# A four-layer attention and expert kernel: other steps for layer 0's exps and experts, more matmuls on ones, an int4 maximum by a transpose, other steps for layer 3's norm and last outputs

## The chip, the cores and the metric

The kernel runs on one core of a Trainium2 chip. The metric is the device time of one execution in microseconds. Three executions of the kernel before were timed, and one more was profiled. TensorE is called PE in the profile, VectorE DVE, ScalarE ACT, GpSimd POOL and SyncE SP; PEld is TensorE's weight load, which runs beside its matmuls.

## The reference

The input x has 16 sequences of 256 tokens of 128 numbers: 4096 tokens. There are four layers, each of the form `x = x + attention(xn) + ffn(xn)` with `xn` the layer norm of x.

```python
# layer 0: 16 heads of 8; each sequence keeps the 76 keys of largest importance
importance = relu(xn @ wi1.T + bi1) @ wi2.T + bi2
out = softmax(q k / sqrt(8), over the kept keys) @ v @ wo.T + bo
# its ffn: 8 experts, each takes the 512 tokens with its largest gate
top_scores, sel = top_k(softmax(xt @ wg).T, 512)
h = silu(routed @ w1) * (routed @ w3);  out[sel] += h @ w2
# layer 1: 16 heads of 64, causal mask of a window of 32 and 64 global tokens;
#   ffn: the two best of 8 experts for each token, relu squared
# layer 2: 4 heads of 32 with a distance mask that depends on the query; ffn of width 512, two gelus
# layer 3: 16 heads of 64, causal;  ffn: a matrix quantized to int4, plus a low-rank term
scale = max(|kernel|) / 7
w = clip(round(kernel / scale), -8, 7) * scale
y = xn @ w + bias + (xn @ a) @ b
```

## The kernel before, in words

All numbers are float32. The 4096 tokens are eight chunks of 512 (`NC = 8`), each of four tiles of 128 tokens. x stays on chip from layer to layer. The order of the work is written out by hand, in numbered steps, and each engine executes its instructions in the order in which the program issues them: an instruction that waits holds up everything behind it on its engine.

**PSUM** has eight banks: two tiles "sc" of two banks each, two "tp" of one, one "mm" and one "po". A tile is free again when its readers are done. `mm1()` gives the single "mm" bank, so every user of it waits for the one before; layer 0's `bank()` goes round "tp" and "mm".

**Layer 0** (`Layer0.run`) runs steps kk from -8 to 67, eight to a chunk (c = kk // 8, r = kk % 8). An even step issues `exps`: 16 matmuls of keys by queries (L817) into two "sc" tiles and two ACT exponentials (L823). An odd step issues `maxima` of the next chunk (16 matmuls L783 and four DVE reductions L789). Then come, as the step asks, `queries` (transposes of the maxima, L803, and a DVE addition L808), `outputs` of the exps one step earlier (L834, copied by ACT at L840), `divided` (transposes L849), `turned` (L864), `project` (L874, DVE addition L878) and `value` (L766). After these the step advances its lanes, which are generators: `prelude` (the choice of keys for a chunk two ahead, its ranking on DVE at L708 and L712), `choice` (15 rounds of a search for the experts' thresholds: a DVE comparison ge L485, matmuls L491 that count, DVE L496 to L502) and one `expert` for each e, which starts at step 19 + 3e. An expert builds one-hot tiles on DVE (L576, in two steps), multiplies them (L597) to get its token numbers (L605 to L610), gathers its rows with four indirect DMAs on POOL's queue (L613), scales them by their gates on DVE (L623), transposes them (L629), runs the two matrices (L638, silu L642, product L643), the third one (L648), copies the result y with ACT (L653; one buffer), and adds the rows to a tensor in HBM with four indirect DMAs on POOL's queue (L662). `fetch` reads that tensor back on SP's queue, `finish` (L998, POOL) adds it to the attention's result, and `Route.early` begins layer 1's norm (`stat`, `root`, `apply` L1292, `turn` L1298) while layer 0 ends. `warm(n)` issues n matmuls of a tile of ones by itself (L373), whose result nobody reads; they stand where TensorE would have little to do.

**Layers 1 and 3** share `Pipeline.slots`: NU = 128 slots u, each a pair of heads of one sequence. Two slots make one round: scores (L1110), DVE minima (L1125), ACT exps (L1136), POOL division (L1145), transposes (L1155) with DVE copies eT (L1156), values (L1169), projections of later heads (L1082, L1095). `out_half` multiplies eight tiles of heads by the output matrix into the "mm" bank (L1187; in layer 3 first L1185 with the int4 matrix) at slots with u % 8 equal to 1 and 5. `norm_steps` computes layer 3's norm of the next chunk from slot u % 16 == 3 on, one piece to a slot: statistics in two slots, root, POOL's `xn` (L1051) in two slots, and then transposes into the "mm" bank (L1059) and a copy by ACT (L1061). In layer 1, `Route` runs beside it: `places` works out where each token goes, `scatter` writes rows (64 indirect DMAs), `blocks` runs the experts on blocks of rows from slot 49 on, `gather` reads rows back from slot 93 on. From slot 56 on, `aside` advances small things for later layers by one step a slot, among them `quantized`: the int4 matrix. It takes the maximum of each row on DVE, and the maximum over the 128 partitions with `partition_all_reduce` on POOL (L1984).

**Layer 2** runs block by block; in its last one, layer 3's generator is advanced at hand-picked places (`beside`), so that layer 3's first norm is done there.

Of the kernel before, what the change touches and what calls it, by code (L numbers as in the profile page):

```python
# [19 lines left out]
P = 128  # L20
# [202 lines left out]
class Layer0:  # L223
# [245 lines left out]
    def choice(self):  # L469
# [9 lines left out]
        for i in range(15):  # L479
# [7 lines left out]

            self.warm(12 if i < 2 else 4)
            pc = self.bank()[:, : 3 * NE * 8]
# [80 lines left out]
    def expert(self, e):  # L570
# [31 lines left out]
        nc.scalar.activation(fourths, pix[:, :P], AF.Copy)  # L602
        yield

        nc.tensor.matmul(pix[:, P : P + 8], lhsT=fourths, rhs=self.eighths, start=True, stop=True)  # L605
# [12 lines left out]
        yield  # L618
        if e % 2 == 0:

            yield

# [257 lines left out]
    def begin(self):  # L880
# [36 lines left out]
        for _ in lane:  # L917
# [5 lines left out]
        return {  # L923
            -8: [(self.stats, 6, 2, 6), (self.stats, 7, 2, 6), (self.root, 2, 6), (self.apply, 2), (self.apply, 3), warm],
            -7: [
# [7 lines left out]
    def run(self, tail):  # L933
# [7 lines left out]

        warm = {kk: 5 for kk in range(-8, 4)} | {kk: 2 for kk in range(12, 22)} | {kk: 3 for kk in range(53, 64)}
        loads = 19 + 3 * NE + 8
        for kk in range(-8, 8 * NC + 4):
            c, r = kk // 8, kk % 8
            if r == 0 and 0 <= c + 2 < NC:
                lanes.insert(0, self.prelude(c + 2))
                next(lanes[0])
            if 0 <= c < NC and r % 2 == 0:
                self.exps(c, r // 4, r // 2 % 2)  # L950
            if 0 <= c + 1 < NC and r % 2:
# [15 lines left out]
            if r >= 6 and 0 <= c + 1 < NC:  # L967
                self.value(c + 1, r - 6)
            if kk == 45:

                self.pg = self.k.po()
# [39 lines left out]
class Pipeline:  # L1011
# [25 lines left out]
    def norm_steps(self, c):  # L1037
# [12 lines left out]
        for t in range(TT):  # L1050
            nc.gpsimd.tensor_scalar(  # L1051
                xn[:, t, :], x[:, t, :], mv[:, t, 0:1], y[:, t : t + 1], ALU.subtract, ALU.mult
            )
            if t == 1:
                yield
        yield
        pt = k.mm1()
# [120 lines left out]

    def out_half(self, s, t, wo, first=None):

        k, nc = self.k, self.k.nc
        p = k.mm1()
        if first is not None:
            t0 = s % 2 * S + t * P
            nc.tensor.matmul(p[:, :D], lhsT=self.xnT[s // 2][:, t0 : t0 + P], rhs=first, start=True, stop=False)  # L1185
        for n in range(8):
            nc.tensor.matmul(  # L1187
                p[:, :D], lhsT=self.oT[s][:, n, t * P : (t + 1) * P], rhs=wo[:, n, :],
                start=(first is None and n == 0), stop=(n == 7),
            )  # L1190
        return p[:, :D]

    def slots(self, extra, mid=None):

        if self.own:
            yield
            yield from self.norm_steps(0)
            yield
# [55 lines left out]
class Route:  # L1254
# [71 lines left out]
    def early(self):  # L1326

        at = {}
        for first, n in ((0, 2), (2, 2), (4, 2), (6, 1)):
            for c in range(first, first + n):  # L1330
                u = 57 + c + c // 6
                at.setdefault(u, []).append((self.stat, c, first, n))
                for late, step in ((0, self.apply), (1, self.turn)):
                    at.setdefault(59 + c + late, []).append((step, c))
        at[64].append((self.gates, 0))
# [5 lines left out]
    def last(self):  # L1341
        c = NC - 1
        yield
        self.stat(c, c, 1)
        yield
        self.root(c, 1)
        self.apply(c)
        yield
        self.turn(c)
        yield  # L1350
        self.gates(c - 3)
        yield
        self.others(c - 3)
# [198 lines left out]
def layer1(k, wk_, w, route, l2, aside, warm):  # L1552
# [15 lines left out]
    def extra(u):  # L1568
# [9 lines left out]
        next(first, None)  # L1578
        for g, at, n in ((0, 15, 2), (1, 93, 2)):
            if u == at:  # L1580
                rows[g] = route.gather(range(EARLY)) if g else route.scatter()
            if g in rows:
                for _ in range(n):
                    next(rows[g], None)
        if 0 <= u - 49 < NB // 2:
            lanes.append(route.blocks(2 * (u - 49)))
        mid(u)
# [25 lines left out]
class Layer2:  # L1613
# [266 lines left out]
    def run(self, wk_, att, begin, l3, route):  # L1880
# [20 lines left out]
        for n in range(NC + 1):  # L1901
# [38 lines left out]
            beside(1)  # L1940
            do(self.turn, q)
            do(self.first, f, 3)
            beside(1)
            do(self.third, f - 1, 0)
# [26 lines left out]
def quantized(k, pool, a):  # L1971
# [9 lines left out]
    nc.vector.tensor_reduce(m, kw, AX.X, ALU.max, apply_absolute_value=True)  # L1981
    yield
    mx = pool.tile([P, 1], F32, name="q_mx")
    nc.gpsimd.partition_all_reduce(mx, m, P, bass_isa.ReduceOp.max)  # L1984
    yield
    yield
# [4 lines left out]
    yield  # L1991
    q = pool.tile([P, D], F32, name="q_q")
    nc.vector.tensor_scalar(q, kw, inv[:, 0:1], None, ALU.mult)
# [15 lines left out]
def layer3(k, wk_, sh, room, w, xs, out):  # L2009
# [9 lines left out]
    pipe = Pipeline(k, wk_, xs, (w["Wq"], w["Wk"]), w["Wv"], k.causal, home=home)  # L2019
    res = {}  # L2020

    def extra(u):
        for late, t in ((9, 0), (13, 1)):
            s, at = (u - late) // 8, (u - late) % 8
            if at or not 0 <= s < 2 * NC:
                continue
            c, n = s // 2, s % 2 * 2 + t
            if n == 0:
                res[c] = k.xp.tile([P, TT, D], F32, tag="x", name="res")
            p = pipe.out_half(s, t, w["o"], first=w["eff"])  # L2030
            nc.vector.tensor_tensor(res[c][:, n, :], p, w["bias"], ALU.add)
            nc.gpsimd.tensor_tensor(res[c][:, n, :], res[c][:, n, :], xs[c][:, n, :], ALU.add)
            if n == 3:
                nc.sync.dma_start(out[c * CT : (c + 1) * CT, :].rearrange("(t p) d -> p t d", p=P), res[c])

    yield from pipe.slots(extra)
# [154 lines left out]
```

## Time and profile before

| what | value |
|---|---|
| three timed executions | 1952.15, 1945.82, 1943.68 us (median 1945.82) |
| the profiled execution, its time and its span | 1939.03 us, 1937.3 us |
| mean granted TensorE clock in it | 0.985 |
| layer 0's exps, L823 | x64, 61.4 to 355.4 us |
| layer 1's values, L1169 on p_v | x1024, 388.2 to 981.3 us |
| layer 2's blocks, L1811 | x512, 1007.2 to 1389.4 us |
| layer 3's values, L1169 on m | x1024, 1405.8 to 1924.9 us |
| POOL's maximum for the int4 matrix, L1984 | x1, 377 ns, at 657.9 us |
| matmuls on ones, L373 | x346, 1.0 to 374.5 us |
| POOL's gathers of layer 0, L613 | x32, median 956 ns, landing 2.6 us after the issue |
| POOL's scatters of layer 0, L662 | x32, median 1574 ns, landing 3.4 us after the issue |

In the profile, a line such as "x<-a,b" names the tile that is written and those that are read. "idle before" is the time in which an engine did nothing before an instruction, with what ended it. Matmuls overlap: one of 0.27 us can follow its forerunner after 0.11 us, so their pitch is read from start to start. The share of the clock that is granted to TensorE stands in windows as a number from 0 to 1.

### The profile page before, as it was taken

How to read it: one execution, taken by the hardware profiler on the slowest of the kernel's cores; microseconds unless marked ns; L12 is line 12 of the kernel's file. 1: busy time of each engine (PE TensorE's matmuls, PEld its weight loads, DVE VectorE, ACT ScalarE, POOL GpSimd, SP SyncE). 2: the span in 40 equal slices, each digit the busy share in tenths (PEclk: the TensorE clock that was granted, in tenths of full speed). 3: DMA queues.
4: the chain of work that ended last, by engine and by line, in shares of the span. 5: the costliest groups of instructions: out<-in, count | busy, mean ns of one | idle time of the engine just before them, and what ended most of it. 6: DMA issues, size and time to landing. Idle time of an engine off the chain costs nothing.

```text
span 1937.3 us, 39257 instructions
## 1 busy us (share of the span) xinstructions
PE 1850.1 (95%) x13823; PEld 1335.7 (69%) x13823; DVE 1226.1 (63%) x4819; ACT 1052.8 (54%) x3162; POOL 960.8 (50%) x1388
## 2 busy tenths in 40 slices
PE   9998889889999899999999999999999999999998
PEld 5555455568878788887754555555577877877786
DVE  6888664697665555568765555443277667766765
ACT  4334545656666566666644444444466666666664
POOL 4015776337997466565664444421144444444442
PEclk9989999899999999999999999999999999999999
DMA  8500223200014354300010000000000000000000
GB/s 248 145 1 13 30 30 66 74 1 23 33 34 129 101 140 136 88 20 15 16 41 5 9 10 12 12 1 1 1 1 8 1 7 7 7 1 7 7 1 12
DMA packets 83208, 72.28 MB, mean 37 GB/s; under 512 B 14466, under 2 KB 74020, under 8 KB 82852
## 3 DMA queue, kind: packets, MB, share of 16 engines
q1 hardware_dynamic: 66784, 38.01, 6.9%
q0 software_dynamic: 15488, 31.61, 6.7%
q8 instruction: 109, 1.79, 0.4%
q14 instruction: 87, 0.71, 0.1%
q10 hardware_dynamic: 740, 0.17, 0.0%
HBM read 49.70 MB, written 24.25 MB: 38 GB/s over the span
## 4 chain that ended last, share of the span: by engine, by line
PE 64%; DVE 7%; POOL 7%; issue 2%; ACT 1%; POOLq 0%; ACTq 0%; DVEq 0%
PE sc L1811 11%; PE sc L1082 9%; PE po L1169 7%; PE tp L1155 7%; PE sc L1110 7%; PE mm L1187 5%; PE sc L1095 4%; POOL e L1145 3%; POOL xb L1452 2%; DVE e L1125 2%; PE po L1511 2%; PE mm L1498 2%; PE mm L1851 2%; DVE eT L1156 1%; PE sc L1803 1%
## 5 line engine op out<-in xcount | busy, mean ns | idle before, releaser
L1145 POOL TENSOR_TENSOR e<-e,rs 128x256 f32<-128x256 f32 (+2 forms) x512 | 400.0, 807 | 483.1 <-DVE rs L1143 448.3
L1136 ACT ACTIVATE e<-e,mn 128x128 f32<-128x128 f32 (+2 forms) x1024 | 442.4, 434 | 285.8 <-DVE mn L1125 281.8
L1156 DVE COPY eT<-tp 128x384 f32<-128x384 f32 x512 | 261.3, 552 | 59.8 <-PE tp L1155 59.6
L1811 PE MATMUL sc<-ff,h 128*128 128x512 f32 x512 | 227.2, 593 | 1.6 <-DVE l_mn L1738 1.6
L1155 PE MATMUL tp<-ident,e 128*128 128x128 f32 x1536 | 219.0, 278 | 8.6 <-POOL e L1145 5.6
L1175 DVE COPY oT<-po 128x512 f32<-128x512 f32 x128 | 88.3, 690 | 215.8 <-PE po L1169 215.8
L1155 PEld LDWEIGHTS tp<-ident,e 128*128 128x128 f32 x1536 | 173.3, 141 | 61.6 <-issue 37.3
L1136 ACT ACTIVATION_READ_ACCUMULATOR e<-e,mn 128x1 f32 x1024 | 191.9, 187 | 0.0
L1811 PEld LDWEIGHTS sc<-ff,h 128*128 128x128 f32 x512 | 94.4, 190 | 106.4 <-issue 101.2
L1125 DVE CUSTOM_DVE_ANT_0 e<-sc,causal 128x128 f32<-128x128 f32 (+1 forms) x512 | 151.8, 353 | 11.2 <-PE sc L1110 10.8
L1125 DVE CUSTOM_DVE_ANT_0 e<-sc,sparse 128x128 f32<-128x128 f32 (+1 forms) x512 | 138.8, 328 | 7.2 <-POOL dist L183 2.2
L1082 PE MATMUL sc<-m,qkv 128*128 128x256 f32 x512 | 126.8, 390 | 1.7 <-DVE mn L1125 1.7
L1691 POOL TENSOR_SCALAR n<-dist,reach 128x128 f32<-128x128 f32 (+1 forms) x128 | 119.2, 931 | 16.4 <-DVE l_mn L1738 5.0
L1187 PE MATMUL mm<-out,oT 128*128 128x128 f32 x1024 | 124.9, 275 | 0.0
L1187 PEld LDWEIGHTS mm<-out,oT 128*128 128x128 f32 x1024 | 119.4, 192 | 0.1
L1790 POOL TENSOR_TENSOR x<-l_o,x 128x256 f32<-128x256 f32 x16 | 11.6, 727 | 199.7 <-DVE l_o L1784 199.3
L1082 PEld LDWEIGHTS sc<-m,qkv 128*128 128x128 f32 x512 | 92.5, 190 | 17.0 <-DVE mn L1125 2.3
L1110 PE MATMUL sc<-n 64*128 64x128 f32 (+1 forms) x1024 | 101.5, 337 | 1.3 <-ACT n L1087 0.8
L1169 PE MATMUL po<-eT,p_v 128*64 128x256 f32 (+1 forms) x1024 | 99.4, 333 | 2.0 <-DVE eT L1156 1.9
L1169 PE MATMUL po<-eT,m 128*64 128x256 f32 (+1 forms) x1024 | 98.1, 332 | 0.4 <-DVE eT L1156 0.4
L1169 PEld LDWEIGHTS po<-eT,p_v 128*64 128x64 f32 x1024 | 63.9, 136 | 43.7 <-issue 16.3
L1742 ACT ACTIVATE p_e<-p_e,l_mn 128x128 f32<-128x128 f32 (+1 forms) x128 | 56.3, 441 | 68.3 <-DVE l_mn L1738 68.1
(433 smaller groups left out, 3686.6 us busy)
## 6 DMA issues: line engine op xcount, KB each, us to landing
xb<-zero SPq DMA_DIRECT2D x1, 4608.0 KB, 20.4
xb<-xb SPq DMA_DIRECT2D x36, 128.0 KB, 2.8
yb<-yb SPq DMA_DIRECT2D x36, 128.0 KB, 2.3
x<-in_L_attn_x SPq DMA_DIRECT2D x8, 256.0 KB, 3.8
m<-in_L_ffn_w SPq DMA_DIRECT2D x8, 256.0 KB, 11.3
xn_d<-x SPq DMA_DIRECT2D x8, 256.0 KB, 8.0
m<-acc_d SPq DMA_DIRECT2D x8, 256.0 KB, 5.4
h<-in_L_ffn_h_wT SPq DMA_DIRECT2D x2, 1024.0 KB, 7.5
```

The lines of the kernel that those rows point to most:

```text
L1082: nc.tensor.matmul(p[:, n, i * S : (i + 1) * S], lhsT=self.wqk[n][:, (2 * gg + i) * P : (2 * gg + i + 1) * P], rhs=(self.xk if n else self ...
L1110: nc.tensor.matmul(ps[:, j, c0:c1], lhsT=qk[r, 0, i, qt * P : (qt + 1) * P], rhs=qk[r, 1, i, k0 : k0 + c1 - c0], start=True, stop=True,)
L1125: nc.vector.tensor_tensor_reduce(out=e[:, j, c0:c1], in0=ps[:, j, c0:c1], in1=self.mask[:, c0:c1], scale=1.0, scalar=3e38, op0=ALU.add, op ...
L1136: nc.scalar.activation(e[:, j, c0:c1], e[:, j, c0:c1], AF.Exp, bias=mn[:, n], scale=-1.0, accum_out=sums[:, n])
L1145: nc.gpsimd.tensor_tensor(e[:, :, c0:c1], e[:, :, c0:c1], bcast(rs[:, 2 * qt : 2 * qt + 2], 2, c1 - c0), ALU.mult)
L1155: nc.tensor.transpose(pt[:, n * P : (n + 1) * P], e[:, j, c0 : c0 + P], k.ident)
L1156: nc.vector.tensor_copy(eT[:, j, :], pt[:, :384])
L1169: nc.tensor.matmul(o[64 * j : 64 * j + 64, t * P :], lhsT=v[:, t ^ self.swap, h : h + 64], rhs=eT[:, j, t * S : t * P + S], start=(t == 0) ...
L1175: nc.vector.tensor_copy(self.oT[s][:, 2 * gg : 2 * gg + 2, :].rearrange("p i s -> p (i s)"), self.po.pop(g))
L1187: nc.tensor.matmul(p[:, :D], lhsT=self.oT[s][:, n, t * P : (t + 1) * P], rhs=wo[:, n, :], start=(first is None and n == 0), stop=(n == 7),)
L1691: self.nc.gpsimd.tensor_scalar(mk[:, j, c0:c1], self.k.dist[:, c0:c1], reach[:, g, t : t + 1], 1e18, ALU.is_gt, ALU.mult)
L1811: self.nc.tensor.matmul(ph, lhsT=self.w[wh][:, c, m * P : (m + 1) * P], rhs=src[c], start=(c == 0), stop=(c == NF - 1))
```

## The change

1. Layer 0: `exps` is issued behind the transposes and matmuls of an even step instead of ahead of them. An odd expert waits one step before it works out its numbers and gathers, and then has two free steps instead of one before it scales; an even expert keeps its steps. The fetches begin two steps later, as does the use of "po" for the ones of the end.
2. More ones: 28, 12 and then 7 in the rounds of `choice` instead of 12, 12 and then 4; 25 instead of 3 in step -8; 5 instead of 2 in steps 12 to 16.
3. `turn` of layer 1's early norm comes two steps after `apply` instead of one (also in `Route.last`), and scatter, blocks and gather begin one slot later.
4. `quantized` takes the maximum over the partitions by a DVE copy of the column to 128 columns, one PE transpose and a DVE maximum.
5. Layer 3's `norm_steps` has an empty slot between POOL's last piece and the transposes; its first norm starts one `beside` earlier, and one `beside` of layer 2 comes one block earlier.
6. Layer 3's result tile is begun by POOL with x plus the bias (one instruction of 128x512 for a chunk instead of four of 128x128 behind the DVE addition). The outputs of the last sequence are begun in slots 126 and 127 with six of eight tiles of heads, in the "mm" and a "tp" bank, and finished in slot 128.

```diff
@@ choice
-            self.warm(12 if i < 2 else 4)
+            self.warm((28, 12, 7)[min(i, 2)])
@@ expert
         nc.scalar.activation(fourths, pix[:, :P], AF.Copy)
         yield
+        if e % 2:
+            yield
...
         yield
         yield
-        if e % 2 == 0:
-
-            yield
+
+        yield
@@ Layer0.begin, run
-            -8: [..., (self.apply, 3), warm],
+            -8: [..., (self.apply, 3), (self.warm, 25)],
...
-        warm = {kk: 5 for kk in range(-8, 4)} | {kk: 2 for kk in range(12, 22)} | {kk: 3 for kk in range(53, 64)}
-        loads = 19 + 3 * NE + 8
+        warm = {kk: 5 for kk in range(-8, 4)} | {kk: 5 for kk in range(12, 17)} | {kk: 2 for kk in range(17, 22)} | {kk: 3 for kk in range(53, 64)}
+        loads = 19 + 3 * NE + 10
...
-            if 0 <= c < NC and r % 2 == 0:
-                self.exps(c, r // 4, r // 2 % 2)
...
             if r >= 6 and 0 <= c + 1 < NC:
                 self.value(c + 1, r - 6)
-            if kk == 45:
+            if 0 <= c < NC and r % 2 == 0:
+
+                self.exps(c, r // 4, r // 2 % 2)
+            if kk == 47:
@@ norm_steps, before its transposes
+        yield
         yield
         pt = k.mm1()
@@ slots
         if self.own:
-            yield
             yield from self.norm_steps(0)
@@ Route.early
-                    at.setdefault(59 + c + late, []).append((step, c))
+                    at.setdefault(59 + c + 2 * late, []).append((step, c))
@@ Route.last
         self.apply(c)
+        yield
         yield
         self.turn(c)
@@ layer1
-        for g, at, n in ((0, 15, 2), (1, 93, 2)):
+        for g, at, n in ((0, 16, 2), (1, 94, 2)):
...
-        if 0 <= u - 49 < NB // 2:
-            lanes.append(route.blocks(2 * (u - 49)))
+        if 0 <= u - 50 < NB // 2:
+            lanes.append(route.blocks(2 * (u - 50)))
@@ Layer2.run
             do(self.turn, q)
+            beside(1)
             do(self.first, f, 3)
-            beside(1)
@@ quantized
+    q = pool.tile([P, D], F32, name="q_q")
+    nc.vector.tensor_copy(q, m.to_broadcast([P, D]))
+    yield
+    pm = k.mm1()
+    nc.tensor.transpose(pm[:, :P], q, k.ident)
     mx = pool.tile([P, 1], F32, name="q_mx")
-    nc.gpsimd.partition_all_reduce(mx, m, P, bass_isa.ReduceOp.max)
-    yield
+    nc.vector.tensor_reduce(mx, pm[:, :P], AX.X, ALU.max)
     yield
@@ out_half
-    def out_half(self, s, t, wo, first=None):
+    def out_half(self, s, t, wo, first=None, p=None, upto=8):
-        p = k.mm1()
-        if first is not None:
+        begun = p is not None and upto == 8
+        if p is None:
+            p = k.mm1()
+        if first is not None and not begun:
...
-        for n in range(8):
+        for n in range(6, 8) if begun else range(upto):
@@ layer3, extra
+        if u == NU - 2:
+            last.append(k.mm1())
+        if u == NU - 1:
+            last.append(k.tp())
+        if u in (NU - 2, NU - 1):
+            pipe.out_half(2 * NC - 1, u - NU + 2, w["o"], first=w["eff"], p=last[-1], upto=6)
...
             if n == 0:
+
                 res[c] = k.xp.tile([P, TT, D], F32, tag="x", name="res")
+                nc.gpsimd.tensor_tensor(res[c], xs[c], bcast(w["bias"], 1, TT), ALU.add)
             p = pipe.out_half(s, t, w["o"], first=w["eff"])
-            nc.vector.tensor_tensor(res[c][:, n, :], p, w["bias"], ALU.add)
-            nc.gpsimd.tensor_tensor(res[c][:, n, :], res[c][:, n, :], xs[c][:, n, :], ALU.add)
+            nc.vector.tensor_tensor(res[c][:, n, :], p, res[c][:, n, :], ALU.add)
...
+        if u == NU:
+            c = NC - 1
+            for t in range(2):
+                p = pipe.out_half(2 * NC - 1, t, w["o"], p=last[t])
+                nc.vector.tensor_tensor(res[c][:, 2 + t, :], p, res[c][:, 2 + t, :], ALU.add)
+            nc.sync.dma_start(out[c * CT : (c + 1) * CT, :].rearrange("(t p) d -> p t d", p=P), res[c])
```

## The prediction

> **What bounds the kernel now.** I read the page first, then the chain of waits, then windows and timelines around each place that the change touches.
>
> ```profile
> span 1937.3 us, 39257 instructions
> PE 1850.1 (95%) x13823; PEld 1335.7 (69%) x13823; DVE 1226.1 (63%) x4819; ACT 1052.8 (54%) x3162; POOL 960.8 (50%) x1388
> PEclk9989999899999999999999999999999999999999
> PE 64%; DVE 7%; POOL 7%; issue 2%; ACT 1%; POOLq 0%; ACTq 0%; DVEq 0%
> ```
>
> TensorE is 95% busy and 64% of the chain, so a microsecond in which it stands still is mostly a microsecond of the total. The clock row dips only in its first fifth. Windows of one microsecond show it at 0.50 from 30.0 to 36.9, 112.0 to 118.8, 135.9 to 142.7, 176.8 to 183.7 and 347.5 to 354.3 (6.8 us each), at 211, 252, 272 and 378 (3.4 us each), and from 664.9 to 671.8. All but the last lie in layer 0 or at its end. So the change is a sum over TensorE's gaps and its half-clock stretches.
>
> **Part 1, the int4 maximum (layer 1's slot 60).** The timeline of that place:
>
> ```profile
> 657.87 0.38 POOL L1984 PARTITION_ALL_REDUCE q_mx<-q_m  x1 [5.76 <-issue]
> 666.01 1.44 POOL L1145 TENSOR_TENSOR e<-e,rs 128x256 f32<-128x256 f32 x2 [7.77 <-issue]
> 666.67 0.47 PE L1155 MATMUL tp<-ident,e 128*128 128x128 f32 x1 [4.78 <-POOL e L1145]
> ```
>
> The reduction takes 0.38 us, but POOL stands idle 5.76 us before it and 7.77 us after it, with nothing to wait for; TensorE then waits 4.78 us for POOL's division L1145 and falls to half clock. Windows from one pair of slots to the next (cut where the first L1169 of a pair starts) give the price:
>
> ```profile
> core 0: us, PE busy (x) PEld busy (x) DVE busy (x) ACT busy (x) POOL busy (x), PEclk, DMA share, GB/s
> 654.48:673.09 18.61, 13.46 (x94) 11.52 (x93) 9.00 (x31) 7.34 (x24) 6.65 (x10) 0.82 0.24 66
> 686.89:697.75 10.86, 10.86 (x93) 9.51 (x92) 6.44 (x25) 7.34 (x24) 5.47 (x9) 1.00 0.35 102
> ```
>
> The same work takes 18.61 instead of 10.86: 7.75 us. The next pair takes 13.80 where its like take 12.65; I count half of that 1.15, since the int4 steps stay in it: 8.3. What comes instead: a DVE copy of 128x128 (about 0.3, as L1577), one transpose (0.11 from start to start) and a DVE maximum. The transpose needs the single "mm" bank just after ACT's L1504; the like case is L2003, which waited 0.5 us for it. The maximum's own wait holds up DVE's next oT copy, which comes later than that anyway. Net **-7.7**, between -9 and -6.
>
> [...]
>
> **Part 2, layer 3's norm one step later.** Slots of the first chunk with this step, TensorE, then ACT:
>
> ```profile
> 1500.09 0.38 PE L1059 MATMUL mm<-ident,m 128*128 128x128 f32 x2
> 1500.77 0.33 PE L1059 MATMUL mm<-ident,m 128*128 128x128 f32 x1 [0.30 <-POOL m L1051]
> 1501.55 0.33 PE L1059 MATMUL mm<-ident,m 128*128 128x128 f32 x1 [0.44 <-POOL m L1051]
> 1501.71 1.89 PE L1082 MATMUL sc<-m,qkv 128*128 128x256 f32 x8
> 1504.10 0.39 PE L1185 MATMUL mm<-weff,m 128*128 128x128 f32 x2
> ...
> 1501.91 0.60 ACT L1061 ACTIVATE m<-mm 128x512 f32<-128x512 f32 x1 [0.82 <-PE mm L1059]
> 1504.16 1.00 ACT L1087 ACTIVATE n<-sc 128x1024 f32<-128x1024 f32 x1
> ```
>
> The last two transposes wait for POOL: starts 0.56 and 0.78 apart instead of 0.11, so 1.1 us. In all, seven chunks have a pair of 10.65 us against 9.13. One step later POOL is done. But step 9 also starts an output half (L1185), which uses the same single bank: its first matmul now waits for ACT's copy of the transposes, and that copy now stands behind step 8's exps and L1087. Worked out: without the step, L1082 starts at 1500.1; in a pair without a norm, L1087 ends 3.95 us after L1082 starts (1483.84 to 1487.79), so at 1504.05; plus 0.60 for the copy, 1504.65. Without a wait, transposes and outputs would stand at 1503.05. The new stall is about 1.6 against 1.1 now: +0.5 a chunk, seven times **+4**. Behind it in TensorE's queue stand L1095 and L1169, so nothing fills it. If ACT comes 0.5 sooner it is 0; 1 us later, +8.
>
> Before layer 3 proper, the same copy (1370.43) held TensorE's L1851 by 1.4 us; now block 3 of "first" (3.44 us) lies between: **-1.4**.
>
> **Part 3, the last outputs.** The end:
>
> ```profile
> 1930.21 0.29 DVE L2031 TENSOR_TENSOR res<-mm,bias 128x128 f32<-128x128 f32 x1 [2.37 <-PE mm L1187]
> 1930.58 0.45 POOL L2032 TENSOR_TENSOR res<-res,x 128x128 f32<-128x128 f32 x1 [2.21 <-DVE res L2031]
> 1931.06 0.37 SPq L2034 DMA_DIRECT2D out_dram<-res  x1
> ```
>
> Fourteen of the eighteen last matmuls go ahead of the last values, into idle time: from 1921.39 to 1930.17 TensorE idles about 1.9, of which I let 0.8 stay (the copy L1175 of 0.69 and its wait). POOL's 0.48 leaves the end. **-1.5**, between 0 and -3. POOL's four additions of 0.45 become one of 128x512 (1.26, as L998) ahead of the DVE addition, in POOL's queue behind a division; in step 9 that ends near when TensorE's half does, and DVE has slack: 0.
>
> **Part 4, layer 0.** Its TensorE gaps sum to 39.9 us, not all curable. Four rows:
>
> ```profile
> 32.03 1.46 PE L425 MATMUL tp<-ident,x 128*128 128x128 f32 x4 [3.39 <-ACT x L411]
> 176.83 1.12 PE L629 MATMUL mm<-ident,xr 128*128 128x128 f32 x4 [2.80 <-DVE qa L808]
> 228.07 0.69 DVE L623 TENSOR_TENSOR xr<-xr 128x512 f32<-128x512 f32 x1 [4.21 <-DMA xr<-xn_d,ids]
> 250.30 0.60 ACT L653 ACTIVATE y<-tp 128x512 f32<-128x512 f32 x1 [6.65 <-DMA acc_d<-y,ids]
> ```
>
> *Ones.* 92 more (22 at step -8, 16+39 in the choice, 15 in steps 12 to 16) at 0.11 from start to start are 10 us. The 22 (2.4 us) sit before the 3.39 us gap; the 16 before a wait of 2.34 for DVE's ge; the others beside a VectorE that is 85% busy. What stays on the path, I put at 1 to 2. They can save the stretches at 30, 112 and 136. [...] A stretch of 6.8 us costs at most 3.4, as half the matmuls go through. I take -1 for the first and -1.5 net for each of the others: **-4**, between -8 and +2.
>
> *Experts.* An odd expert's gather is issued one step later, its scaling (L623) two. Now the scaling of experts 3, 5 and 7 waits 4.2, 3.0 and 3.0 for the gather, because POOL has an expert's four scatters (about 7.7 us) ahead of it in the same slot; after, the gather goes first. TensorE lost 2.1 by the first, under 1 by the others: -3. The wait of ACT's copy y for the previous scatters (4.76 and 6.65; TensorE's part 1.8 and 2.7) moves from four pairs of experts to three: -1. The 2.80 before 176.83 hangs on VectorE's order, which stays. The last scatters end two slots later; SP's fetch (324.1, POOL adding from 327.0 to 334.8) moves with its users, two slots of 2.5. **-4**, -10 to +6.
>
> *Exps behind the transposes.* Work of 0.4 to 1.7 us goes ahead of exps that wait 7.6 us in all for banks; behind, the outputs have 1.2 to 6 us of slack after ACT's exps until slot 54, but only 0.05 to 0.6 later. Saved perhaps 2, lost perhaps 2: **0**, -3 to +4. Turns one slot later cure waits of 1.3 and 2.5 on ACT, but ACT itself waits there for VectorE's root: 0. The shifts by one slot in layer 1 (64 row scatters on POOL, the blocks' fetches on SP and weight gathers on POOL, 24 gathers) move together, each behind the same neighbours: 0, ±2.
>
> **Sum.** -7.7 +4 -1.4 -1.5 -4 -4 = -14.6. From the profiled execution's 1939.0 (span 1937.3 and 1.7 around it) 1924.4; the median shown is 1945.8, 6.8 higher, and I predict there: **1931**.
>
> **Rivals.** (a) *POOL takes over in layer 0, slower.* Slots 32 to 35 now hold a gather, scatters, a gather, scatters: 25 us of POOL (a gather about 5) in 23 (slots of 5.8). If ACT's y in slots 34, 40 and 46 waits a full 7.7 plus 3.4 to land, TensorE stops 4 to 5 us and then runs a 6.8 us stretch at half (3.4 lost): 7 to 8 for each pair, +23 for three and the -4 gone: 1958. From 5 us a pair on, it cancels all the rest. For it: ACT waited 6.65 so already. Against: two of four pairs had no such wait. (b) *Only the reduction's gain remains.* The ones save no stretch (+4), experts nothing (+4), the norm costs +8 (+4): 1943. For it: the single bank. (c) *Layer 0 gains more*: all its stretches at half clock after 112 go (another 10): 1921. Against: those at 176 and 347 begin with waits that stay.
>
> **Chances and range.** Forecast 0.58, (a) 0.12, (b) 0.17, (c) 0.13. The part bounds give 1916 to 1946 around the forecast; reaching into (a) and (c), 1913 to 1952. A change under 0.5% (9.7 us) can't be told from none: faster by more than that 0.69, within 0.18, slower 0.13.
>
> **What would show it.** No PARTITION_ALL_REDUCE and no second stop; the pair near 655 at about 11.5. L1185's first matmul with a wait for ACT in seven chunks, those pairs at 11 or more: if they are 10 or less, Part 2 is wrong. L623 without waits for DMA; 438 ones instead of 346, no half clock at 112 and 136. ACT's y waiting over 7 us three times would mean (a).

## The result and the profile after

| kernel | median (lowest to highest) | ratio to before, 95% interval | profiled span |
|---|---|---|---|
| before | 1945.77 us (1943.68 to 1952.15) | | 1937.3 us |
| changed | 1954.7 us (1951.35 to 1961.9) | 1.0046 [1.003, 1.0062] | 1952.0 us |

The changed kernel is 0.46% slower, 9 us, and the interval leaves out 1. The forecast was 1931 us. The first lines of its page:

```profile
span 1952.0 us, 39365 instructions
PE 1864.2 (96%) x13916; PEld 1346.7 (69%) x13916; DVE 1227.6 (63%) x4821; ACT 1052.2 (54%) x3162; POOL 959.2 (49%) x1363
PEclk9999897999999999999999999999999999999999
```

TensorE is busy for 14.1 us more, about the whole difference of the spans. The 92 more ones take some 8 of them. Busy time also holds what matmuls lose at half clock (the 16 of L818 take 1.10 us at full clock, at 59.69, and 2.00 at 0.50, at 309.80), but that explains little here: before the last issue the changed kernel spends 58.0 us at 0.50, the kernel before 54.6. I did not trace the rest. The clock row has its dip of 7 in the seventh slice, from 293 to 342 us, where the kernel before shows a 9.

Where the time goes is seen by taking the same matmul in both traces and subtracting its starts. Positive means that the changed kernel is late. I call this number the lag.

| same work | before, us | changed minus before, us |
|---|---|---|
| layer 0, exps of step 20 | 148.0 | -2.9 |
| step 42 | 277.8 | -6.9 |
| step 48 | 309.1 | +0.7 |
| step 52 | 321.0 | +10.9 |
| step 60 | 342.5 | +19.2 |
| layer 1, first values | 388.2 | +16.9 |
| the pair before the int4 pair | 641.8 | +17.2 |
| behind the int4 pair | 673.1 | +10.2 |
| layer 1, last pair | 980.1 | +13.5 |
| layer 3, first values | 1405.8 | +13.5 |
| layer 3, pair 62 | 1919.9 | +17.9 |
| end | 1937.3 | +14.7 |

Everything behind layer 0 sums to 14.7 - 16.9 = -2.2 us. All of the loss, and more, is in layer 0, and there between steps 42 and 60.

The int4 maximum did what was forecast. Windows of the changed kernel over the pair ahead of it and the pair that had taken 18.61 us:

```profile
core 0: us, PE busy (x) PEld busy (x) DVE busy (x) ACT busy (x) POOL busy (x), PEclk, DMA share, GB/s
659.01:672.46 13.45, 12.98 (x111) 11.39 (x110) 6.72 (x28) 7.29 (x24) 8.37 (x11) 1.00 0.47 135
672.46:683.32 10.86, 10.86 (x93) 9.51 (x92) 7.58 (x31) 7.34 (x24) 5.59 (x8) 1.00 0.40 106
```

The second pair is at its usual 10.86, without half clock. The first takes 13.45 against 12.65; this 0.80 is the price of the copy, the transpose and the maximum, and it is the same 13.45 in e4, which makes this change alone.

Layer 3's norm gives the stall that the prediction named. The timeline of the changed kernel in the first such chunk:

```profile
1516.90 0.60 PE L1062 MATMUL mm<-ident,m 128*128 128x128 f32 x4
1517.38 1.00 ACT L1090 ACTIVATE n<-sc 128x1024 f32<-128x1024 f32 x1
1518.28 0.58 ACT L1064 ACTIVATE m<-mm 128x512 f32<-128x512 f32 x1
1518.91 0.49 PE L1190 MATMUL mm<-weff,m 128*128 128x128 f32 x2 [1.41 <-ACT m L1064]
```

The four transposes follow each other without a wait, ACT copies their bank only behind its copy L1090, and the first output matmul waits 1.41 us for the bank. The same wait of 1.40 to 1.41 stands in all seven chunks.

In layer 0, ACT's copy y of expert 6 waits in step 46, and TensorE waits behind it. Timeline of the changed kernel:

```profile
308.11 0.60 ACT L654 ACTIVATE y<-tp 128x512 f32<-128x512 f32 x1 [4.98 <-DMA acc_d<-y,ids]
308.60 0.38 ACT L841 ACTIVATE ov<-mm 128x256 f32<-128x256 f32 x1
308.76 1.11 PE L850 MATMUL tp<-ident,ov 128*128 128x128 f32 x4 [2.79 <-ACT y L654]
```

ACT waits for the scatters of expert 5, which is now only two steps ahead of expert 6. TensorE's transposes of ov wait behind it, and from 308.17 to 321.8 the granted clock is 0.50. That looked like the answer; the experiments say that it is at most a part of it.

### The profile page after: what moved, and what is told of

It reads as the page before. It is cut to its first block, busy times and chain, and to the rows that moved or that the text cites. A ratio compares the mean times of both kernels' runs of the same rounds, so it can differ in the third digit from the quotient of the medians.

```text
span 1952.0 us, 39365 instructions
## 1 busy us (share of the span) xinstructions
PE 1864.2 (96%) x13916; PEld 1346.7 (69%) x13916; DVE 1227.6 (63%) x4821; ACT 1052.2 (54%) x3162; POOL 959.2 (49%) x1363
## 4 chain that ended last, share of the span: by engine, by line
PE 65%; DVE 6%; POOL 6%; ACT 2%; issue 1%; ACTq 0%; DVEq 0%
PE sc L1816 11%; PE sc L1085 9%; PE po L1172 8%; PE sc L1113 7%; PE tp L1158 7%; PE mm L1192 5%; PE sc L1098 4%; POOL xb L1457 3%; POOL e L1148 2%; PE mm L1503 2%; PE po L1516 2%; PE mm L1856 2%; PE sc L1808 1%; PE sc L1809 1%; DVE e L1128 1%
## 5 line engine op out<-in xcount | busy, mean ns | idle before, releaser
L1113 PE MATMUL sc<-qk 64*128 64x128 f32 (+1 forms) x1024 | 92.1, 320 | 5.9 <-ACT qk L1090 5.9
```

The costliest lines, as they stand in the source:

```text
L1113: nc.tensor.matmul(ps[:, j, c0:c1], lhsT=qk[r, 0, i, qt * P : (qt + 1) * P], rhs=qk[r, 1, i, k0 : k0 + c1 - c0], start=True, stop=True,)
```

## The experiments

Each ratio is to the kernel before, timed beside the run. One thousandth of a ratio is 1.95 us. The medians of e8, e11, e16 and e18 rest on 6 or 7 executions, the others on 11 to 22. "Layer 0" is my estimate of layer 0's part of the difference: ratio minus 1, times 1946, less what the later layers differ in the two profiles; the sign ± gives half the width of the ratio's interval. e4 and e8, whose layer 0 is the kernel before's, stand at 0 and -2 in it, which is how well the estimate does.

| run | edit | median, us | ratio [95%] | layer 0, us |
|---|---|---|---|---|
| e1 | changed, exps ahead | 1948.67 | 1.0010 [1.0001, 1.0019] | +4 ±2 |
| e2 | changed, old experts | 1949.15 | 1.0014 [0.9993, 1.0035] | +5 ±4 |
| e3 | changed, old norm step | 1953.86 | 1.0029 [1.0019, 1.0039] | +12 ±2 |
| e4 | before + int4 | 1939.62 | 0.9966 [0.9957, 0.9976] | 0 ±2 |
| e5 | changed, exps ahead, old experts | 1944.98 | 0.9992 [0.9978, 1.0005] | 0 ±3 |
| e6 | before + exps | 1945.57 | 1.0001 [0.9988, 1.0015] | -2 ±3 |
| e7 | before + experts | 1951.67 | 1.0023 [1.0011, 1.0035] | +3 ±2 |
| e8 | before + int4 + end | 1938.30 | 0.9949 [0.9931, 0.9968] | -2 ±4 |
| e9 | changed + second y | 1951.15 | 1.0037 [1.0019, 1.0055] | +9 ±4 |
| e10 | before + exps + experts | 1954.53 | 1.0051 [1.003, 1.0073] | +11 ±4 |
| e11 | e8 + exps before step 44 | 1927.86 | 0.9916 [0.9884, 0.9947] | -8 ±6 |
| e12 | e8 + second y | 1933.95 | 0.9944 [0.993, 0.9958] | -3 ±3 |
| e13 | before + exps from step 44 | 1953.80 | 1.0042 [1.0026, 1.0059] | +7 ±3 |
| e14 | before + ones | 1945.46 | 1.0002 [0.9988, 1.0015] | +1 ±3 |
| e15 | changed, exps ahead from step 44 | 1953.05 | 1.0028 [1.0014, 1.0042] | +7 ±3 |
| e16 | e11 + second y | 1929.84 | 0.9919 [0.9899, 0.994] | -8 ±4 |
| e17 | e13 + late ones | 1946.91 | 1.0009 [0.9993, 1.0026] | +2 ±3 |
| e18 | e11 + experts 1 and 3 | 1930.91 | 0.9926 [0.9903, 0.9949] | -6 ±5 |
| changed | | 1954.7 | 1.0046 [1.003, 1.0062] | +11 ±3 |

### Undoing one part of the change: e1, e2, e3, e5

e1 undoes the move of the exps, e2 the experts' steps (with the fetches and the bank), e5 both.

```diff
 e1
+            if 0 <= c < NC and r % 2 == 0:
+                self.exps(c, r // 4, r // 2 % 2)
             if 0 <= c + 1 < NC and r % 2:
                 self.maxima(c + 1, r // 2)
...
-            if 0 <= c < NC and r % 2 == 0:
-
-                self.exps(c, r // 4, r // 2 % 2)
 e2
         nc.scalar.activation(fourths, pix[:, :P], AF.Copy)
         yield
-        if e % 2:
-            yield
...
-        yield
+        if e % 2 == 0:
+            yield
...
-        loads = 19 + 3 * NE + 10
+        loads = 19 + 3 * NE + 8
...
-            if kk == 47:
+            if kk == 45:
 e3, norm_steps
         yield
-        yield
+        if not c:
+            yield
         pt = k.mm1()
```

> The changed kernel with layer 0's exps issued ahead of the transposes again; all else as changed. In the profiles the changed kernel is 6.9 us ahead of the kernel before at the exps of step 42 and 19.2 behind at those of step 60: 26 us are lost in between. Theory A (the place of the exps: outputs, divided and the clock wait for ACT's later exps): without it most of the 26 does not arise, the exps of step 60 come within 5 us of the kernel before or earlier, and the time is about 1933 (1928 to 1940). Theory B (the experts' steps: experts 5 and 6 now follow each other by two steps, and y of step 46 waits for scatters): the loss stays, the time is 1950 to 1957. Theory C (the two together: each alone is harmless): about 1935 here and in the run with the old expert steps.

> The changed kernel with the experts' old steps (odd ones gather a step earlier and scale two steps earlier, fetches at the old step, the last ones in po two steps earlier); all else as changed. Theory A (exps): the loss of 26 us between steps 42 and 60 stays but for a few us: 1948 to 1955. Theory B (experts): it goes, and the time is about 1933 (1928 to 1940); y of ACT in step 46 has no wait for a scatter, and TensorE no 13.7 us at half clock from step 48 on. Theory C (both needed): about 1935.

> The changed kernel without the empty step in layer 3's norm for the chunks after the first. In the profiles the changed kernel loses 0.6 to 0.8 us in each of seven chunks there, 4.4 in all. Theory: the first output matmul with the int4 matrix stops waiting for ACT's copy of the transposes, the transposes wait for POOL again, and the time falls by 4.4 to about 1950. Rival: the loss in those chunks comes from the outputs' other order (POOL's addition of 128x512 ahead of the division) and stays: 1954 to 1955.

> The changed kernel with both the old place of the exps and the old steps of the experts; more ones, later turns and layer 1's shifts stay. So far each undone alone brought about 6 us. Theory add (two separate losses): both together bring 12 to 14, 1941 to 1944. Theory interaction (the loss needs both, or what is left of it has one more cause in layer 0, the ones): 1947 to 1949. The layers after layer 0 are as in the changed kernel: 3.4 us gained in layer 1, 4.4 lost in layer 3, 3 gained at the end.

No theory about e1 and e2 had it whole: each of them brings 6 to 7 us by the ratios. The lag of 16.9 us at the end of layer 0 is larger than the 11 of the table because the kernel before was profiled in an execution 6.8 us under its median, and the changed kernel in one only 1.0 under its own. e5 lands at 1945.0, just above the range of "add" and far from that of "interaction". From step 48 to 60 its trace is 0.1 us off the kernel before.

e3's median fell by only 0.8 us, and its ratio by 3.3, so the trace has to decide. Its lag stays at 18.7 us from layer 3's first values to pair 62, where the changed kernel's went from 13.5 to 17.9. The norm's step costs 4.4 us, once 0.8 and six times 0.6; the rival (POOL's addition, which e3 keeps) is out.

### Doing one part alone: e4, e6, e7, e8, e10, e14

These are the kernel before with the hunks of the change: e4 `quantized`; e6 the exps; e7 the experts; e8 `quantized` with `out_half` and layer 3's `extra`; e10 exps and experts; e14 the ones.

> The kernel before with the int4 maximum by a transpose alone. Theory (prediction, part 1): POOL's two stops of 5.76 and 7.77 us and the half clock at 665 go, and 7.7 us with them: 1938. [...]

> The kernel before with layer 0's exps issued behind the transposes and matmuls of their step, nothing else. Prediction: 0 (-3 to +4), 1943 to 1950. Theory A2 (in the last steps, behind nothing but ones, the next odd step finds the banks of the exps full and ACT late, 1.5 us a pair of steps instead of 0.9 or less): +5 to +8, 1951 to 1954, lost from step 44 on.

> The kernel before with the experts' new steps alone. Prediction: -4 (-10 to +6), 1942. Theory B2 (experts 5 and 6 now follow each other by two steps, y in step 46 waits 5 us for scatters, TensorE 2.8, a stretch at half clock follows, and the end of expert 7 comes two steps later): +5 to +8, 1951 to 1954, lost from step 46 to 52.

> The kernel before with two parts of the change alone: the int4 maximum by a transpose and the last outputs begun early with POOL's addition first. Theory: 7.7 for the maximum and about 3 at the end (in the profiles the changed kernel is 17.9 behind before its last values and 14.7 at its end): 1935 (1934 to 1937). Rival (the end gains only because TensorE is late there anyway, the prediction's 1.5 or less): 1937 to 1938.5.

> The kernel before with the exps behind the transposes and the experts' new steps, and the old number of ones. Alone, the first gave 1945.6 against 1946.0 and the second 1951.7; the changed kernel's layer 0, with more ones too, is about 11 us slower by its median (9 of the whole, and 2 for what the later layers gain). Theory add (no interaction): 1951 to 1952. Theory interaction of the two (the shifted experts meet exps that come late): 1955 to 1958. If it is the first, the ones are the third part of the loss.

> The kernel before with the 92 more ones alone. Prediction: -4 (-8 to +2), 1941. Theory W (the ones fill 3 us of gaps ahead of step 12 and take 8 themselves, and what they save of the half clock pays for about the rest): 0 to +2, 1945 to 1947, with less half clock in the profile of layer 0 than the kernel before's 24 to 31 us.

e4: 6.4 us by the medians; the profile goes from 6.1 behind to 0.85 ahead over the two pairs, 6.9 us.

e8: from the pair ahead of the last values to the end the lag falls by 3.3 us, 5.6 to 2.3, as in the changed kernel (17.9 to 14.7). The median of 1938.3 lies in the rival's range and the ratio (9.9 us) in the theory's, so the times cannot tell them apart. The trace can: over the same stretch e4, which lacks the new end, gains 0.0.

e6 gives 0, as predicted and against theory A2, but as a sum of two large terms: its profile is 3.2 us ahead at step 48 and 5.8 behind at step 60. e7 is slower by 5.7 us by the medians (in the range of theory B2) and by 4.5 by the ratio, where the prediction had a gain. It has the wait for y too (5.39 us in step 46). Its edit also holds the later fetches and the later use of "po"; no run separates these. e14 gives 0. e10 gives +9.9, between its two theories. That is 5.3 us more than e6 and e7 together, with ±5.5 from the three intervals. The same sum inside the changed kernel (changed - e1 - e2 + e5) leaves 2.7 ±6. So an interaction of a few us is likely, and neither comparison alone is clear of noise.

By the cost of half clock I mean half of the time spent at 0.50: a stretch of 6.8 us counts 3.4. In e14's profile it is 25.6 us in layer 0, against 23.9 in the kernel before and 29.0 in e4, whose layer 0 is the kernel before's: the ones saved none that can be told. Before step 12 TensorE's gaps fall from 11.0 to 5.7 us while the ones take 40.9 instead of 33.5, so 2 us are lost there.

### A second buffer for y: e9, e12

```diff
-        y = p2.tile([P, 4, D], F32, tag="y", name="y", bufs=1)
+        y = p2.tile([P, 4, D], F32, tag="y", name="y", bufs=2)
```

> The changed kernel with two buffers for y instead of one, so that ACT's copy y of one expert no longer waits for the scatters of the expert before; nothing else. In the changed kernel ACT waits 4.98 us for that in step 46 (5.2 to 5.4 in the other runs with the experts' new steps), TensorE 2.8 behind it, and a stretch of 13.7 us at half clock begins 0.6 us before that copy. Theory Y (this wait is where the experts' new steps lose): the wait goes, and 5 to 9 us with it: 1946 to 1950. Rival (the loss is the end of expert 7, two steps later, beside the last exps): under 2 us, 1953 to 1956.

> The kernel before with the int4 maximum by a transpose, the last outputs begun early, and two buffers for y. In the kernel before ACT's copy y waits for scatters 4.8, 6.7 and 3.5 us in three of eight experts; TensorE's part was 1.8 and 2.7 in two of them. Theory Y: those and some time at half clock behind them go: 1931 to 1935. Rival (a later thing holds the same work, as DVE, or the clock takes it back): 1937 to 1939.

In e9 no y waits for a scatter any more (the longest wait left is 0.96 us, for its matmuls), and still its profile loses 17 us between steps 48 and 60. The ratio falls by 0.0009, 1.8 us with ±4.7; the median, 1951.15, lies between theory and rival. So the wait that looked like the answer is not where most of the time goes. (The stretch at half clock begins with that copy, at 308.17 against 308.11, and not 0.6 us ahead of it as the expectation has it.) In e12 the median, 1933.95, is in the range of theory Y, but the ratio is 0.9944 against e8's 0.9949, 1 us: no difference that can be told.

### Which steps of the exps: e11, e13, e15, e16

```diff
 e11 (with e8's hunks), e16 (with a second y too)
-            if 0 <= c < NC and r % 2 == 0:
+            if 44 <= kk < 8 * NC and r % 2 == 0:
                 self.exps(c, r // 4, r // 2 % 2)
             if 0 <= c + 1 < NC and r % 2:
                 self.maxima(c + 1, r // 2)
...
                 self.value(c + 1, r - 6)
+            if 0 <= kk < 44 and r % 2 == 0:
+                self.exps(c, r // 4, r // 2 % 2)
 e13: the two conditions exchanged, nothing else; e15: e11's in the changed kernel
```

> The kernel before with the int4 maximum by a transpose, the last outputs begun early, and the exps behind the transposes in the steps before 44 alone, ahead of them from step 44 on. With the exps behind in all steps the profile was 3.2 us ahead at step 48 and lost 9.0 from there to step 60. Theory (the place costs only in the late steps, and gains before them): 3 us under the run without it (1938.3), 1934 to 1936. Rival (the 3.2 us were the chance of one profile's clock): 1938 to 1939.

> The kernel before with the exps behind the transposes in the steps from 44 on alone. Theory (the place of the exps costs only there): in the profile 9 us are lost between steps 48 and 60, of them 9 to 12 in all runs with the exps behind so far and 0 in all without; the time is 1952 to 1956. Rival (the loss needs the early steps' order too): 1945 to 1948.

> The changed kernel with one edit: from step 44 on the exps are issued ahead of the transposes again. Theory (late place costs 9 to 12, early place gains 3 to 5): more than the 6 us which the old place brings in all steps: 1940 to 1945; between steps 48 and 60 the profile loses 3.6 us of moved work and 4 to 6 of the experts, no more. Rival (the early place gains nothing beside the new experts' steps): 1947 to 1950.

> The kernel before with the int4 maximum by a transpose, the last outputs begun early, the exps behind the transposes before step 44, and two buffers for y. The same without the second buffer gave 1927.9 in six runs, the same with the second buffer and the old exps 1934.0. Theory: the gains add in part, 1925 to 1929. Rival (the six runs were lucky; both take the same waits away): 1930 to 1934.

The move in the late steps alone costs 0.42%, as e13's theory had it. In the early steps alone it brings 0.33% over e8, more than expected, and beside a second y 0.25% over e12 (both pairs of intervals overlap a little); e16's median lies between its theory and its rival. Windows from step 48 to 52, to 60, and to layer 1's first values, first of e11 (exps ahead in these steps; the kernel before has 11.90 and 21.51 in the first two):

```profile
core 0: us, PE busy (x) PEld busy (x) DVE busy (x) ACT busy (x) POOL busy (x), PEclk, DMA share, GB/s
308.61:320.50 11.89, 11.07 (x131) 7.55 (x130) 5.56 (x12) 7.06 (x9) 8.15 (x10) 1.00 0.31 28
320.50:342.00 21.50, 19.53 (x217) 11.34 (x213) 10.49 (x34) 10.30 (x15) 8.57 (x7) 1.00 0.43 106
342.00:389.55 47.55, 39.88 (x266) 25.62 (x265) 29.48 (x158) 31.07 (x83) 17.82 (x35) 0.86 0.26 75
```

and of e13 (exps behind), in the same columns:

```profile
313.47:326.72 13.25, 11.24 (x131) 7.39 (x131) 6.00 (x13) 7.11 (x10) 8.89 (x10) 1.00 0.32 27
326.72:356.57 29.85, 25.43 (x215) 14.64 (x214) 12.52 (x47) 10.21 (x15) 7.68 (x7) 0.77 0.28 73
356.57:397.47 40.90, 33.70 (x261) 22.13 (x260) 26.85 (x143) 30.69 (x82) 17.50 (x35) 1.00 0.31 88
```

In the middle window the same work takes 8.35 us more, and the granted clock is 0.77 instead of 1.00: 29.85 times 0.23 is 6.9 us of clock, not all of it paid, since TensorE waits in part of that time anyway. The gaps (window less PE busy) grow from 1.97 to 4.42, so by 2.5. In the last window e13 gets 6.7 back, where its clock is 1.00 and e11's 0.86.

Why the gaps grow is in the timelines. In e11, the transposes L849 follow the exps and lie beside ACT:

```profile
320.50 1.76 PE L817 MATMUL sc<-qa,ka 32*76 32x256 f32 x16
322.20 0.66 PE L849 MATMUL tp<-ident,ov 128*128 128x128 f32 x4
323.04 0.53 PE L783 MATMUL sc<-ka,q 32*128 32x152 f32 x4 [0.19 <-ACT a_p L823]
```

In e13 they come first (the view starts at the last of the four), and the maxima, which need the banks of the exps, wait with nothing in between:

```profile
326.52 0.27 PE L849 MATMUL tp<-ident,ov 128*128 128x128 f32 x1
326.72 1.10 PE L817 MATMUL sc<-qa,ka 32*76 32x256 f32 x16
328.99 0.53 PE L783 MATMUL sc<-ka,q 32*128 32x152 f32 x4 [1.17 <-ACT a_p L823]
```

The edit moves the wait rather than removing it: it takes TensorE's cover away from ACT's time.

e15 is a miss for its theory and its rival. It recovers 3.5 us by the ratio, not 9 to 12, and is no better than e1. So the early place, worth about 5 us beside the old experts (e11 against e8 6.5, e16 against e12 4.9), is worth nothing beside the new ones (e15 against e1: 3.5 us slower, the intervals overlap a little).

The profiles of all runs but e17 and e18 can be sorted by two choices, the place of the exps and the experts' steps. The table gives how much the lag grows; its third column goes by the place of the exps before step 44, its fourth by that from step 44 on. For the new experts it counts from the same work: expert 7's first matmuls (3.6 us) stand behind step 48 there and are moved back.

| exps | experts | step 20 to 48, us | step 48 to 60, us |
|---|---|---|---|
| ahead | old | 0.0 to 9.5 (before, e4, e5, e8, e12, e13, e14) | 0.0 to 0.1 (before, e4, e5, e8, e11, e12, e14, e16) |
| behind | old | -1.6, 0.7, 2.8, 4.0 (e16, e6, e11, e2) | 9.0, 9.7, 12.3 (e6, e13, e2) |
| ahead | new | 5.7, 6.1 (e1, e7) | 4.2, 6.3, 9.1 (e1, e7, e15) |
| behind | new | 4.8 to 12.8 (e15, changed, e10, e3, e9) | 11.3 to 14.9 (e10, e3, e9, changed) |

From step 48 to 60 both moves cost, and together no more than their sum. From step 20 to 48 the move of the exps gains beside the old experts and not beside the new ones; but the profiles of the first row, whose exps and experts are the same there, spread over 9.5 us, so this is a tendency.

### What the late place is paid in: e17; and the experts 1 and 3: e18

```diff
 e17, on e13
+            if 46 <= kk < 8 * NC and kk % 2 == 0:
+                self.warm(8)
-            if warm.get(kk):
+            elif warm.get(kk):
                 self.warm(warm[kk])
 e18, on e11
         yield
+        if e in (1, 3):
+            yield
...
-        if e % 2 == 0:
+        if e % 2 == 0 or e < 4:
             yield
```

> As the run with the exps behind in the steps from 44 on alone (1953.8; its profile lost 9.7 us between steps 48 and 60, of which TensorE's gaps are 3.6 and stretches at half clock 6.8), with 8 ones behind the exps of each even step from 46 on instead of 0 or 3: 57 more ones, some 6 us of them. Theory clock (the gaps for ACT are short, most of the price is the half clock that sets in over them): the ones lie in the gaps, the half clock between steps 48 and 60 goes, and those steps lose 3 to 5 us instead of 9.7: 1947 to 1950. Rival (the ones delay what waits for nothing, or the clock falls all the same): 1953 to 1957.

> As the run with the int4 maximum, the last outputs and the exps behind before step 44 (1927.9), with the new steps for experts 1 and 3 alone; 5 and 7, the fetches and the bank stay as they were. Theory late (the experts' new steps lose at experts 5 to 7, in steps 43 to 52, and gain by the gathers of 3 before): 1924 to 1928. Theory early (beside exps that come behind, the new steps lose at every odd expert): 1930 to 1934.

e17 costs 0.09% instead of 0.42% (the intervals touch), with 57 matmuls more than e13. Its window over step 52 to 60:

```profile
323.74:347.49 23.75, 21.67 (x238) 13.18 (x237) 12.49 (x47) 10.19 (x15) 7.75 (x7) 1.00 0.34 91
```

It is 6.1 us shorter than e13's, and its clock is 1.00. So the late place is paid for mostly in clock, and the ones buy it back where they lie in a wait. e18's median, 1930.9, is in the range of "early", but it decides nothing against e11's 1927.9: the intervals overlap widely.

## Why the prediction was wrong

In the later layers each term can be read off the traces, because the same code repeats within 0.1 us there; layer 0 is taken from the ratios:

| step of the sum | predicted, us | measured, us |
|---|---|---|
| Part 1, int4 maximum | -7.7 | -6.9 (-7.7 in its pair, +0.8 in the one ahead) |
| Part 2, norm in seven chunks | +4 | +4.4 |
| Part 2, L1851 at the head | -1.4 | -1.6 (the wait is gone; the lag falls from 15.2 to 13.65 there) |
| Part 3, last outputs | -1.5 | -3.2 |
| shifts by one slot in layer 1 | 0 ±2 | +3.5 in all (+1.2, +1.8 and +1.4 at three pairs, the rest smaller and both ways) |
| Part 4, layer 0 | -8 | +11 ±3 by the ratio, +16.9 in the profile |

Parts 1 and 2 hold in mechanism and nearly in size. The pair of the maximum is even 0.6 us better than the 11.5 that the prediction asked for, and the pairs of the norm take 11.24, "11 or more" as it asked. At the end the sum was too small by what the last section tells. Layer 1's shifts, left at zero, are +3.5: in the pair that ends at 836.9 one more block's matmuls (L1503, L1516) stand than in the kernel before; the other two pairs I did not follow. Not in the table is a stretch of 3.4 us at half clock at 1038.6, which the kernel before's profile lacks: +1.7 in layer 2.

**The step that failed is Part 4**, by 19 us. By the ratios the experts' term is off by 8.5 us and the ones' by 4.4. What is left, about 6, is what the moved parts do together, for which the sum had no term. The term of the exps came true, but by luck.

*Exps, "0, -3 to +4".* The prediction had seen that there is slack until slot 54 and next to none later, and it priced that as 2 against 2. It counted the gaps and left out the clock. In e13 the late steps cost about 8 us by the ratio; in its profile 9.7 are lost between steps 48 and 60, with gaps of 3.6 us and about 7 of clock, and 4.8 come back behind step 60. The early steps bring about 5, not 2, with the old experts. That the two cancel alone (e6) is why "0" came true there, for the wrong reason.

*Experts, "-4, -10 to +6".* Alone they cost 4.5 (e7). The three waits of the scaling for the gather are gone as predicted: the kernel before lost 10.3 us of DVE there, the changed one nothing. ACT's y waits 3.75, 0.91 and 4.98 instead of 4.76, 6.65 and 3.5. But by e9 this wait, rival (a)'s mechanism, is not the main price: without it the loss from step 48 to 60 stays. Rival (a) had the sign and nearly the size, 1958, and not the cause; it asked for three waits over 7 us, and there is none. What in the experts' steps costs the 4.5 stays open. In e7 it lies in steps 48 to 60 (6.3 us, of which 5.1 are half clock).

*Ones, "-4".* They give 0 (e14). The count, 438, is right. The stretches at 30, 112 and 136 are gone in the changed kernel, but that was no saving of theirs to count: e4, with the same layer 0 as the kernel before, has none at 112 and 136 either, and one of 10.2 us at 144.9 and one of 17.1 at 213.2 instead. No run shows the 1 us and twice 1.5 us that the sum took for these stretches: e14's profile loses 25.6 us to half clock in layer 0, the kernel before's 23.9. The prediction treated the stretches of one execution as fixtures of the code.

*What the parts do together* had no term. In layer 0, e5, without the moved exps and experts, costs 0 ±3, exps alone -2 ±3, experts alone +3 ±2, and both with the ones +11 ±3. The profiles put the difference between steps 20 and 48, where the moved exps lose their gain beside the moved experts. That it is there is likely (see e10), and which instruction carries it the runs don't show.

Two more things hurt. The profiled execution lay 6.8 us under the median, and e4's and e8's profiles, with the same code there, reach layer 1 5.7 and 10.2 us later and lose 29.0 and 30.7 us to half clock instead of 23.9. And the range was too narrow by the prediction's own numbers: the bounds of its parts, added up, give 1909 to 1960 and not 1916 to 1946. The measured 1954.7 lies inside the former.

No long gap stood right ahead of some of the stretches. In the 10 us before the stretch at 112.0, the longest gap of TensorE in the kernel before is 1.03 us (L491 at 109.67, for DVE's ge); e13's first late stretch begins at 330.8, and the longest gap in the 10 us before is 1.17.

**A version that beats both** is e11: the int4 maximum, the last outputs and the exps behind only before step 44, at 1927.9 us. It is 0.84% [0.53, 1.16] faster than the kernel before; e16, with a second buffer for y and at 1929.8 us, is 0.81% [0.6, 1.01] faster.

## What to carry to other kernels

A step that looks free because a consumer has slack must be judged at the place where the slack is smallest. Count the clock with the gaps: here 3.6 us of new gaps came with about 7 us of half clock, and matmuls on ones, put into the wait itself, took most of the loss away (0.09% in e17 instead of 0.42% in e13). Do not count the half-clock stretches of a single execution as savings: look at what a second execution of the same code shows. Change the schedule of two interleaved streams one at a time: here the exps alone cost nothing, the experts alone 4.5 us, and both together about 10.

## What the hardware showed that I had not expected

Within one execution the stretches at half clock lie on one grid: in layer 0 of the kernel before they begin at 30.1, 112.0, 135.9, 176.8, 211.0, 251.9, 272.4, 347.5 and 378.2, whose distances are 24, 7, 12, 10, 12, 6, 22 and 9 times 3.41 us, and each lasts one or two such units; in the changed kernel the first nine, from 168.2 on, are 4, 10, 5, 13, 9, 8, 3 and 14 units apart and last one to four. The grid's place differs between executions. e17 and e13 have the kernel before's code up to step 44. e17's grid lies as the kernel before's, within 0.02 us, and up to there it has stretches at 112.0, 135.9, 176.8, 211.0 and 272.4 again, and reaches step 44 at the same time; e13's lies 0.38 us later, and it has stretches at 112.3, 146.5, 180.6, 255.7 and 276.2 and is 4.3 us late there.

The grid also shows what stands ahead of half clock. I cut all twenty profiles into its units of 3.41 us, up to the last outputs. All 81 units at full clock in which TensorE is busy under 40% are followed by half clock, of 768 between 40% and 80% 124 are, and of 10,072 above 80% only 3. In e13 between steps 52 and 60, units with 55%, 76% and 70% precede its three stretches; in e17 no unit there is under 83%. This is counted from traces and was not tried by itself, and it does not tell how long a stretch lasts.

The end of the program seems to depend on POOL. In all eight profiles where POOL's addition is the last work (the kernel before, e4, e6, e7, e10, e13, e14, e17) the span ends 6.25 us after the last output is issued; in the twelve where DVE's is (the others), 3.63 to 3.65. The last lines of the changed kernel's timeline:

```profile
1947.52 0.29 DVE L2055 TENSOR_TENSOR res<-mm,res 128x128 f32<-128x128 f32 x1 [0.81 <-PE mm L1192]
1947.96 0.29 DVE L2055 TENSOR_TENSOR res<-tp,res 128x128 f32<-128x128 f32 x1 [0.15 <-PE tp L1192]
1948.32 0.37 SPq L2056 DMA_DIRECT2D out_dram<-res  x1
```

The transfer itself lands after 2.3 to 2.4 us in both kernels. So 2.6 of the 3.2 us gained at the end come after the last output's issue, which Part 3 had no term for; what it did count, 1.5, brought 0.6. That a late POOL instruction holds the end is what the twenty profiles suggest, not something that was tried by itself.
